# A fused Perceiver block: the last 65 keys of each batch in the first cross-attention, split into 64 keys and one row

## The chip, the core and the metric

The kernel runs on one core of a Trainium2 chip. A core has five engines with a queue of instructions each: TensorE (PE in the profile; PEld is its weight load), VectorE (DVE), ScalarE (ACT), GpSimd (POOL) and SyncE (SP), which here only issues DMAs. ScalarE issues some DMAs too. Each engine runs its instructions in order and waits on semaphores for the others. Products are summed in PSUM, in eight banks of 128 partitions by 512 f32. The metric is the device time of one execution in microseconds, the median over runs.

## The reference

Two layers on a state `x` of 8 batches by 64 queries by 512, with a context of 8 x 1601 keys by 512, all in f32. The first layer has a cross-attention, an attention over low frequencies, and a routed feed-forward; the second a cross-attention, an attention with relative positions, and a feed-forward with quantised weights. The part that the change concerns is the first cross-attention:

```python
HEADS = 16
DIM_HEAD = 64
SCALE = DIM_HEAD ** (-0.5)
q = x @ Wq.T
kv = context @ Wkv.T
k, v = jnp.split(kv, 2, axis=-1)
...
sim = jnp.einsum('bhid,bhjd->bhij', q, k) * SCALE
sim = jnp.where(mask[:, None, None, :], sim, max_neg)
attn = jax.nn.softmax(sim, axis=-1)
out = jnp.einsum('bhij,bhjd->bhid', attn, v)
out = out.transpose(0, 2, 1, 3).reshape(B, Nq, HEADS * DIM_HEAD)
return out @ Wout.T + b_out
```

Keys and values have 16 heads of 64. 1601 keys are twelve blocks of 128 and a last one of 65.

## The kernel before

`l0_xattn` computes this without ever making the keys: the queries are multiplied with the key weights first (`qk`, 512 context channels by 8 heads by 64 queries), so that the scores of a block of keys are context columns times `qk`. Likewise the attention is applied to the context rows, and the value weights come after.

The work goes in 17 steps. Step `2b + half` scores batch `b` for one half of the heads (4 pairs of heads by 2 by 64 queries = 512 score columns, `HALF`; `QH` is 256), and, one step late, `attend` applies the softmax of the step before to the context rows. `outputs` (called by `finish`, after the first pair of blocks of the following step) multiplies with the value weights; every fourth step `project` adds a tile to `x`.

*Scores.* The twelve whole blocks are taken in six pairs. `Run.add` makes seven products instead of eight for each 2 x 2 product of a pair (`Quarters.left` and `right_of` make the sums that this needs, on GpSimd). Each product is a `mul` of two 128 x 128 weights by 256 columns (L512). They go into PSUM tiles `x_ps`, `y_ps`, `z_ps` of two banks each; ScalarE (L460, L491) and VectorE (L465) take them out with the mask's bias added, and VectorE keeps the running maximum `m` over keys (L493).

*The tail.* The 65 last keys are scored at the very start of `scores`: `ctxT_tail` holds 512 channels by 128 columns, of which 65 are loaded and 63 are zero, and four products of 128 x 128 by 512 (L505) give `s_ps`, which ScalarE writes into `s[:, LAST]` (L506). The maximum begins with that block. In `softmax` the last block goes first, and its exponentials land in `tail`, 65 rows of which are used: in the sum (L567) and in `outputs` (L661), with the 65 rows of values `v_tail`.

*Values of the tails.* `values_of_tails`, after step 0, makes the value rows of all 520 tail keys: two halves of 512 value columns by five groups of 104 keys (L233), evacuated by ScalarE and written to the DRAM tile `v_tails`, from which each step loads 65 rows.

*PSUM.* `x`, `y`, `z` and `mm` have two banks each. Everything else goes through the two `mm` banks in the order of the program: `s_ps`, the transposed maxima `m_ps` and `top_ps` (held until the softmax's last subtraction), `vt_ps`, `sum_ps` (the softmax's totals, L645, read by a reciprocal at L647), `v_ps` (L652, L661), `o_ps`, and the products below.

*Queries of the later batches.* Batches 0 and 1 have their `qk` made at the start (`keys_side_of_first`). Those of batches 2 to 7 (`REST`, 384 queries) are made by the generator `keys_side_of_rest` in 40 pieces, while steps 1 to 3 run: per pair of heads `g` one piece for the queries (L291, 128 x 128 by 384), and four with two products of 64 x 128 weights each (L278), stored to the DRAM tile `qk_all`. `some(n)` takes the next `n` pieces: two after each pair in `scores`, `2 * part` after each of the four runs in `attend`, and what is left after step 3. After that, pieces of another generator, which prepares ternary weights, are taken one at a time.

*Queues.* The program is written in the order of its steps, but the instructions of each engine are arranged by a planner, which knows what each waits for and has its own times for them; so products of one step can stand between those of another. Loads go through SP. Its order in a step: `qk` of the step, context columns in six pairs (from the input for half 0, and then written to the DRAM tile `kept`, from which half 1 loads them with their sums), `ctxT_tail` for half 0, and later context rows and values. The six `pair` buffers serve columns and rows alike, so a load of columns waits until rows were used. `piece` has two buffers.

Of the kernel before, what the change touches and what calls it, by code (L numbers as in the profile page):

```python
# [10 lines left out]
F32 = mybir.dt.float32  # L11
BF16 = mybir.dt.bfloat16
U8 = mybir.dt.uint8
# [7 lines left out]
P = 128  # L21
# [120 lines left out]
def l0_xattn(K, x, d, ternary, kept):  # L142
# [7 lines left out]
    with ExitStack() as es:  # L150
# [9 lines left out]
        nc.gpsimd.memset(ones, 1.0)  # L160
        ctxT_tail = wp.tile([P, DC, P], F32, tag="ctxT_tail", name="ctxT_tail")
        nc.gpsimd.memset(ctxT_tail, 0.0)
        bias = wp.tile([P, B, NK], F32, tag="bias", name="bias")
# [45 lines left out]

        v_tails = dp.tile([B * TAIL, 2, HALF], F32, tag="v_tails", name="v_tails")  # L210

        def load_columns_tail(b):
            nc.sync.dma_start(
                ctxT_tail[:, :, :TAIL], d["ctxT"][b, :, LAST * P :].rearrange("(c p) n -> p c n", p=P)
            )
# [5 lines left out]

        def values_of_tails():

            n = B * TAIL // 5
            for half in range(2):
                wvT = load_wvT(half)
                for i in range(5):
                    tails = zp.tile([P, B - 2, 2, S], F32, tag="stage", name="tails", bufs=2)
                    tails = tails.rearrange("p b h q -> p (b h q)")[:, : DC * n].rearrange("p (c n) -> p c n", n=n)
                    nc.sync.dma_start(tails, d["tails"][:, ts(i, n)].rearrange("(c p) n -> p c n", p=P))  # L230
                    ps = ps_m.tile([P, HALF], F32, tag="mm", name="vt_ps")
                    for c in range(DC):
                        nc.tensor.matmul(ps[:n], lhsT=tails[:, c, :], rhs=wvT[:, c, :], start=c == 0, stop=c == DC - 1)  # L233
                    vt = piece([2, HALF], "vt")[:n, 0, :]
                    nc.scalar.copy(vt, ps[:n])
                    nc.scalar.dma_start(v_tails[ts(i, n), half, :], vt)

# [44 lines left out]
        def keys_side_of_rest(xnT):  # L282

            for g in range(NG):
# [8 lines left out]
                nc.scalar.mul(qT, ps, 64**-0.5)  # L293
                yield
                for c in range(DC):
                    pair = [ps_m.tile([P, HALF], F32, tag="mm", name="qk_ps")[:, :REST] for _ in range(2)]
                    keys_side(pair, c, w[:, 1, :], qT)
                    stage = zp.tile([P, B - 2, 2, S], F32, tag="stage", name="stage", bufs=2)
                    for h in range(2):
                        K.copy(stage[:, :, h, :], pair[h].rearrange("p (b q) -> p b q", q=S))  # L300
                    nc.sync.dma_start(
                        qk_all[1][:, :, c, g].rearrange("p b h q -> p b (h q)"),
                        stage.rearrange("p b h q -> p b (h q)"),
                    )
                    yield
# [8 lines left out]

        wqT = sp.tile([P, NK, HALF], F32, tag="s", name="wqT")[:, :8, :].rearrange("p (c j) n -> p c (j n)", j=2)
        wk = sp.tile([P, NK, HALF], F32, tag="s", name="wk")[:, :NG, :]
        def load_weights(j):
# [14 lines left out]
        m32 = wp.tile([B * NK, P], F32, tag="m32", name="m32")  # L332
        nc.scalar.dma_start(m8, d["mask"])
        load_columns_tail(0)
        ctxT = load_columns(0)
        place = [tp.tile([P, 4, 3, QH], F32, tag="pt", name="stage").rearrange("p a b q -> p (a b q)") for _ in range(2)]
        qk = wp.tile([P, DC, HALF], F32, tag="qk", name="qk")
        qT = piece([NG, P], "qT")

        def keys_side_of_first(j):  # L340
# [21 lines left out]
        for j in range(2):  # L362
            ps = bank([P, NG // 2, P], "q_ps")
            for i in range(NG // 2):
                for c in range(DC):
# [6 lines left out]
                    )  # L372
            nc.scalar.mul(qT[:, ts(j, NG // 2), :], ps, 64**-0.5)
            if j == 0:
                for _ in keys_side_of_first(0):
                    pass
                now = qk, right_of(qk, nc.vector)
# [6 lines left out]
            bias.rearrange("p b k -> p (b k)"), ps, 1.0, -MASKED, ALU.subtract, ALU.mult  # L384
        )

        def of_weights():
# [64 lines left out]
        class Scores:  # L452
# [29 lines left out]
            def c21(self, ps):  # L482
                if self.k == LAST - 2:
# [6 lines left out]
                    return  # L490
                nc.scalar.activation(self.s[:, self.k + 1, :QH], ps, AF.Identity, bias=self.bias[1], scale=1.0)  # L491
                for k in (self.k, self.k + 1):
                    nc.vector.tensor_max(self.m, self.m if k else self.s[:, LAST, :], self.s[:, k, :])  # L493

        def scores(b, qkt, ctxT):
            qk, qt = qkt
            s = sp.tile([P, NK, HALF], F32, tag="s", name="s")
            m = tp.tile([P, HALF], F32, tag="m", name="m", bufs=1)
# [3 lines left out]
            }  # L502
            ps = ps_m.tile([P, HALF], F32, tag="mm", name="s_ps")
            for c in range(DC):
                nc.tensor.matmul(ps, lhsT=ctxT_tail[:, c, :], rhs=qk[:, c, :], start=c == 0, stop=c == DC - 1)  # L505
            nc.scalar.activation(s[:, LAST, :], ps, AF.Identity, bias=bias[:, b, LAST : LAST + 1], scale=1.0)  # L506
            run = Run()
            for i in range(NPAIR):
# [15 lines left out]
                if i == 0:  # L524
                    finish()
                if i == 3:
                    project()
# [14 lines left out]

        def softmax(s, top):

            parts = []
            for k in (LAST, *range(0, LAST, 2)):
                n = min(2, NK - k)
                nc.vector.tensor_sub(s[:, k : k + n], s[:, k : k + n], top.unsqueeze(1).to_broadcast([P, n, HALF]))  # L548
                if k == LAST:
                    tail = tp.tile([P, HALF], F32, tag="tail", name="tail")  # L550
                    nc.scalar.activation(tail, s[:, LAST, :], AF.Exp)
                    continue
                nc.scalar.activation(s[:, k : k + n], s[:, k : k + n], AF.Exp)  # L553
# [56 lines left out]
        def attend(b, half, soft, ctx):  # L610
# [3 lines left out]
            v_tail = wp.tile([P, HALF], F32, tag="v_tail", name="v_tail")  # L614
            nc.sync.dma_start(v_tail[:TAIL], v_tails[ts(b, TAIL), half, :])
            parts, total, tail = soft
            run = Run()
            for part, right in enumerate(parts):
                pairs = range(3 * part, 3 * part + 3)
                for m in range(2):  # L620
# [12 lines left out]
                    run.add(mul, Mixed(a, m, part == 0))  # L633
                    some(2 * part)
                    next(aside, None)
# [72 lines left out]
        for step in range(2 * B + 1):  # L708
            if step < 2 * B:
                b, half = divmod(step, 2)  # L710
                if step:
                    now, ctxT = queries_of(b, half), load_columns(b, half)
                    if half == 0:
                        load_columns_tail(b)
                s, m = scores(b, now, ctxT)
                top = top_of(m)
# [7 lines left out]
            if step < 2 * B:  # L724
                before = softmax(s, top)
            if step == 0:
                values_of_tails()
            if step == 3:
# [1675 lines left out]
def layout(i):  # L2404
# [11 lines left out]
        "L0x_WqT": i["L0_xattn_Wq"].T,  # L2416
        "L0x_Wk": wkv[:1024],
        "L0x_WvT": wkv[1024:].T,
        "L0x_Wo": i["L0_xattn_Wout"].T,
# [31 lines left out]
        "c_heads": (np.arange(P)[:, None] // DH == np.arange(32)).astype(np.float32),  # L2451
        "L1x_bp": i["L1_xattn_bp"],
        "tails": i["ctx_1024"][:, LAST * P :].transpose(2, 0, 1).reshape(D, B * TAIL),
        "L1x_ln": np.stack(
# [34 lines left out]
```

## Time and profile before

| | |
|---|---|
| median of 3 runs | 2968.94 us (2965.39 to 2969.26) |
| profiled execution, its time | 2970.64 us |
| its span, first to last instruction | 2968.9 us |
| mean granted TensorE clock | 0.992 |
| busy: PE, PEld, DVE, ACT, POOL | 98%, 72%, 61%, 28%, 29% |
| tail scores L505, 16 steps | 128 instructions, 23.0 to 1316.3 us |
| values of tails L233 | 80 instructions, 71.6 to 113.7 us |
| chain that ended last, by engine | PE 92%, DVE 5%, DMA 1%, ACT 1%, issue 1% |

The span holds the whole program; the first cross-attention runs from 0 to about 1445 us. The profile shows one execution, with starts and lengths of instructions; lengths of neighbouring matmuls overlap because matmuls are pipelined, so the cost of one is the distance between starts. A f32 product appears as two instructions.

### The profile page before, as it was taken

The page shows a single profiled execution, that of the slowest core. Times are in us where ns is not written, and L with a number is a line of the kernel's source. Part 1 is how long each engine was busy: PE and PEld are TensorE (multiplying, and loading weights), DVE is VectorE, ACT ScalarE, POOL GpSimd, SP SyncE. Part 2 cuts the span into 40 slices and gives each one's busy share as a digit, 9 for nine tenths or more (in the row PEclk, how much of TensorE's full clock was granted, in tenths as well). Part 3 has the DMA queues.
Part 4 walks back from the last instruction along what each step waited for, and adds up shares of the span by engine and source line. Part 5 has one row for each costly group of instructions (what it writes and reads, how often), then busy time and mean ns, then how long its engine had stood idle before and what let it go on. Part 6 is the DMA issues. An engine that isn't in the chain of part 4 may idle for free.

```text
span 2968.9 us, 39297 instructions
## 1 busy us (share of the span) xinstructions
PE 2912.2 (98%) x15020; PEld 2145.2 (72%) x15025; DVE 1820.5 (61%) x3057; ACT 836.9 (28%) x1566; POOL 860.9 (29%) x766
## 2 busy tenths in 40 slices
PE   8999999999999999999999999999999999999897
PEld 7677778888888888888554445768677677677664
DVE  4565546666666666666533243587667677676738
ACT  2222322233232222222202222232333323323324
POOL 2232241535435252524010003222413404224011
PEclk9999999999999999999999999999999999999989
DMA  9455565554556564542659974202012021120350
GB/s 337 144 184 172 173 213 182 188 199 128 214 173 225 190 211 164 180 144 95 236 199 351 342 236 150 85 26 78 29 67 80 5 92 42 42 92 11 110 83 15
DMA packets 294699, 436.80 MB, mean 147 GB/s; under 512 B 56248, under 2 KB 192448, under 8 KB 291312
## 3 DMA queue, kind: packets, MB, share of 16 engines
q1 hardware_dynamic: 278153, 393.85, 39.9%
q10 hardware_dynamic: 15719, 38.34, 3.7%
q8 instruction: 119, 1.95, 0.3%
q0 software_dynamic: 640, 2.10, 0.2%
q14 instruction: 68, 0.56, 0.1%
HBM read 357.06 MB, written 77.17 MB: 146 GB/s over the span
## 4 chain that ended last, share of the span: by engine, by line
PE 92%; DVE 5%; DMA 1%; ACT 1%; issue 1%; POOL 0%; POOLq 0%; SPq 0%; DVEq 0%; ACTq 0%
PE x_ps L512 11%; PE x_ps L1580 11%; PE x_ps L624 11%; PE y_ps L1580 8%; PE s_ps L1750 6%; PE z_ps L512 5%; PE z_ps L624 5%; PE h_ps L1264 4%; PE oe_ps L1291 4%; PE acc L1809 3%; PE y_ps L512 3%; PE y_ps L624 3%; PE s_ps L505 2%; PE qk_ps L278 1%; PE vt_ps L233 1%; PE v_ps L652 1%
## 5 line engine op out<-in xcount | busy, mean ns | idle before, releaser
L1640 POOL TENSOR_TENSOR r<-r,minus_half 128x52 f32<-128x52 f32 x32 | 276.9, 8672 | 566.4 <-DVE r L1639 566.4
L512 PE MATMUL x_ps<-qt,ctxT 128*128 128x256 f32 x1152 | 285.2, 381 | 2.5 <-DVE s L465 2.5
L624 PE MATMUL x_ps<-pt,ctx 128*128 128x256 f32 x1152 | 273.9, 380 | 0.7 <-DVE a L602 0.7
L136 POOL TENSOR_TENSOR ctx<-ctx 128x256 f32<-128x256 f32 x96 | 78.7, 819 | 621.8 <-DMA ctx<-in_ctx 475.8
L624 PEld LDWEIGHTS x_ps<-pt,ctx 128*128 128x128 f32 x1152 | 217.9, 190 | 40.4 <-DVE a L602 8.2
L512 PEld LDWEIGHTS x_ps<-qt,ctxT 128*128 128x128 f32 x1152 | 217.3, 190 | 40.9 <-issue 6.3
L1750 PE MATMUL s_ps<-qb,kT 128*128 128x256 f32 x832 | 195.6, 382 | 0.0
L1750 PEld LDWEIGHTS s_ps<-qb,kT 128*128 128x128 f32 x832 | 153.6, 190 | 30.5 <-DVE s L1760 8.1
L493 DVE TENSOR_TENSOR m<-m,s 128x512 f32<-128x512 f32 x144 | 110.4, 767 | 67.7 <-ACT s L491 65.6
L1760 DVE TENSOR_TENSOR s<-s_ps,r 128x512 f32<-128x512 f32 x192 | 127.3, 683 | 17.8 <-PE s_ps L1750 16.7
L548 DVE TENSOR_TENSOR s<-s,top_ps 128x1024 f32<-128x1024 f32 (+1 forms) x112 | 123.0, 1135 | 12.0 <-PE top_ps L540 12.0
L1794 DVE TENSOR_TENSOR s<-s,top_ps 128x1792 f32<-128x1792 f32 x64 | 117.9, 1883 | 16.3 <-PE top_ps L1790 16.3
L566 DVE TENSOR_TENSOR total<-total,s 128x512 f32<-128x512 f32 x160 | 117.1, 732 | 4.6 <-DVE total L566 0.5
L465 DVE SCALAR_TENSOR_TENSOR s<-y_ps,bias,p 128x256 f32<-128x256 f32 x96 | 46.3, 483 | 116.2 <-PE y_ps L512 114.9
L1264 PE MATMUL h_ps<-w,tok 128*128 128x512 f32 x256 | 117.3, 593 | 0.0
L1291 PE MATMUL oe_ps<-w,hT 128*128 128x512 f32 x256 | 115.6, 593 | 0.0
L1547 ACT COPY p<-x_ps 128x256 f32<-128x256 f32 (+1 forms) x80 | 33.1, 414 | 282.7 <-PE x_ps L1580 265.4
L1795 ACT ACTIVATE s<-s 128x1792 f32<-128x1792 f32 x64 | 101.3, 1591 | 38.7 <-DVE s L1794 38.7
L553 ACT ACTIVATE s<-s 128x1024 f32<-128x1024 f32 x96 | 100.7, 1057 | 19.0 <-DVE s L548 14.0
L1283 ACT ACTIVATE hT<-hT_ps,L0f_be,L0f_g 128x128 f32<-128x128 f32 x128 | 55.4, 455 | 179.8 <-PE hT_ps L1282 117.0
L1809 PEld LDWEIGHTS acc<-s,v 128*64 128x64 f32 x1664 | 92.3, 139 | 18.3 <-issue 17.0
L1809 PE MATMUL acc<-s,v 128*64 128x128 f32 x1664 | 102.9, 278 | 0.0
(470 smaller groups left out, 6055.3 us busy)
## 6 DMA issues: line engine op xcount, KB each, us to landing
w<-in_L0f_W SPq DMA_DIRECT2D x64, 1024.0 KB
ctx<-in_ctx SPq DMA_DIRECT2D x192, 256.0 KB
kept<-ctxT SPq DMA_DIRECT2D x48, 896.0 KB
ctxT<-kept SPq DMA_DIRECT2D x48, 896.0 KB
ctxT<-kept SPq DMA_DIRECT2D x16, 2688.0 KB
ctxT<-in_ctxT SPq DMA_DIRECT2D x96, 256.0 KB
wvT<-in_L0x_WvT SPq DMA_DIRECT2D x18, 1024.0 KB
qk<-qk_all SPq DMA_DIRECT2D x15, 1024.0 KB
```

Source lines behind the costliest of these rows:

```text
L512: nc.tensor.matmul(ps, lhsT=ctxT[i][:, Quarters.LEFT[n], ts(e, P)], rhs=right[n][:, e, :], start=start and e == 0, stop=e == 1, skip_group ...
L548: nc.vector.tensor_sub(s[:, k : k + n], s[:, k : k + n], top.unsqueeze(1).to_broadcast([P, n, HALF]))
L566: nc.vector.tensor_add(total, total if k > 1 else s[:, 0, :], s[:, k, :])
L624: nc.tensor.matmul(ps, lhsT=ctx[pair][:, Quarters.LEFT[n], ts(m, P)], rhs=right[n][:, i, :], start=start and i == 0, stop=i == 2, skip_gro ...
L1264: nc.tensor.matmul(ps, lhsT=self.tok[:, c, :], rhs=self.w1[n][:, c, :], start=c == 0, stop=c == DC - 1)
L1291: nc.tensor.matmul(ps, lhsT=self.hT[:, f, :], rhs=self.w2[f // 4][:, f % 4, :], start=f == 0, stop=f == 15)
L1580: nc.tensor.matmul(ps, lhsT=left(n, e), rhs=right(n, e), start=start and e == 0, stop=e == 1, skip_group_check=not start,)
L1640: nc.gpsimd.tensor_tensor(r, r, minus_half, ALU.pow)
L1750: nc.tensor.matmul(ps[:, i].rearrange("p h q -> p (h q)"), lhsT=kT[c][:, ts(k0 + i, P)], rhs=qb[c].rearrange("p h q -> p (h q)"), start=Tr ...
L1760: nc.vector.tensor_mul(out, ps, by)
L1794: nc.vector.tensor_sub(part, part, top.to_broadcast([P, n, 2 * P]))
L1809: product = nc.tensor.matmul(acc[ds(64 * j, 64), c, :], lhsT=v[:, k, ds(c * P + 64 * j, 64)], rhs=s[:, k, ts(j, P)], start=k == 0, stop=k ...
```

## The change

The tail's 65 keys become 64 keys and one row, the 1601st key of each batch.

- `tail_scores`: for batches 1 to 7 the 64 keys are scored in products of 64 columns of weights by 256, the first half of the score columns into partitions 0 to 63 of the bank and the second into 64 to 127. Two activations bring both into the step's `tail` tile. Batch 0 keeps one product of 65 keys by 512. The block moves from the start of `scores` to after `finish` in the first pair (for batch 0 it stays at the start). There is no `s[:, LAST]` any more; `tail` (three buffers) is made per step, and the running maximum takes it in after the third pair.
- The 1601st rows: `keys_of_left`, after step 0, makes the key vectors of the eight 1601st rows (`left`), transposes them into `kkT`, with one head of each pair in the upper 64 partitions and the other in the lower, zero elsewhere, and multiplies them with the queries of batch 1 (`qT1`, copied aside by GpSimd). A new piece of `keys_side_of_rest` does so with the queries of batches 2 to 7, for each pair of heads (80 columns of weights by 384, of which 16 rows are kept). `keep_rows` adds the mask's bias `row_bias` and writes them to the DRAM tiles `rows`; `load_row` brings a step's 512 scores of the 1601st key into partition 64 of `tail`, for batches 1 to 7. The products are made for all eight keys and all batches; only those of a batch with itself are loaded.
- `values_of_tails`: 64 keys a batch, four groups of 128 instead of five of 104 per half, and the values of the eight 1601st rows as products of 8 columns by 256.
- `some(2)` after every run of `attend`.

```diff
-        ctxT_tail = wp.tile([P, DC, P], F32, tag="ctxT_tail", name="ctxT_tail")
-        nc.gpsimd.memset(ctxT_tail, 0.0)
+        ctxT_tail = wp.tile([P, DC, TAIL], F32, tag="ctxT_tail", name="ctxT_tail")
...
+        nc.gpsimd.memset(kkT, 0.0)
...
-        def values_of_tails():
-
-            n = B * TAIL // 5
+        def values_of_tails(left):
...
-                for i in range(5):
+                for i in range(B // 2):
...
-                        nc.tensor.matmul(ps[:n], lhsT=tails[:, c, :], rhs=wvT[:, c, :], start=c == 0, stop=c == DC - 1)
-                    vt = piece([2, HALF], "vt")[:n, 0, :]
-                    nc.scalar.copy(vt, ps[:n])
-                    nc.scalar.dma_start(v_tails[ts(i, n), half, :], vt)
+                        nc.tensor.matmul(ps, lhsT=tails[:, c, :], rhs=wvT[:, c, :], start=c == 0, stop=c == DC - 1)
+                    vt = piece([2, HALF], "vt")[:, 0, :]
+                    nc.scalar.copy(vt, ps)
+                    for j in range(2):
+                        nc.scalar.dma_start(v_tails[2 * i + j, :H2, half, :], vt[ts(j, H2)])
+                ps = ps_m.tile([P, QH], F32, tag="mm", name="vl_ps")
+                for c in range(DC):
+                    for n in range(2):
+                        nc.tensor.matmul(
+                            ps[ds(n * H2, B)],
+                            lhsT=left[:, c, :],
+                            rhs=wvT[:, c, ts(n, QH)],
...
+                nc.scalar.dma_start(v_tails[:, H2, half, :], vt)
+
+        ROWS = H2 + 2 * B
+
+        def rows_of(g):
+            return kkT[:, ds(2 * B * g, ROWS)]
+
+        def keys_of_left(left, qT):
+
+            ps = ps_m.tile([P, HALF], F32, tag="mm", name="kl_ps")
+            for c in range(DC):
+                wkT = piece([2, HALF], "wkT")
+                nc.sync.dma_start(wkT, d["L0x_WkT"][ts(c, P), :].rearrange("p (n k) -> p n k", n=2))
+                for n in range(2):
+                    nc.tensor.matmul(
+                        ps[ds(n * H2, B)], lhsT=left[:, c, :], rhs=wkT[:, n, :], start=c == 0, stop=c == DC - 1
+                    )
+            kk = piece([2, HALF], "kk")[:B]
+            for n in range(2):
+                nc.scalar.copy(kk[:, n, :], ps[ds(n * H2, B)])
+            ps = ps_m.tile([P, NG, B], F32, tag="mm", name="kkT_ps")
+            for g in range(NG):
+                nc.tensor.transpose(ps[:, g, :], kk[:, g // 4, ts(g % 4, P)], K.ident[:B, :B])
+            at = kkT[:, :P].rearrange("p (g h b) -> p g h b", h=2, b=B)
+            for h in range(2):
+                nc.vector.tensor_copy(at[ds(h * H2, H2), :, h, :], ps[ds(h * H2, H2)])
+            ps = ps_m.tile([P, NG, S], F32, tag="mm", name="row_ps")
+            for g in range(NG):
+                nc.tensor.matmul(ps[:ROWS, g, :], lhsT=rows_of(g), rhs=qT[:, g, :], start=True, stop=True)
+            keep_rows(ps[: 2 * B].rearrange("p g q -> p (g q)"), rows[0].rearrange("h b g c q -> (h b) (g c q)"))
+
+        def keep_rows(ps, out):
+
+            t = zp.tile([P, HALF], F32, tag="rows", name="rows")[: 2 * B, : ps.shape[-1]]
+            nc.scalar.activation(t, ps, AF.Identity, bias=row_bias, scale=1.0)
+            nc.scalar.dma_start(out, t)
+
+        def load_row(tail, b, half):
+            r = rows[b > 1][:, b, ts(half, NG // 2), b - (2 if b > 1 else 1), :]
+            nc.sync.dma_start(
+                tail[H2:TAIL].rearrange("p (g h q) -> p g h q", h=2, q=S), r.rearrange("h g q -> g h q").unsqueeze(0)
+            )
...
                 nc.scalar.mul(qT, ps, 64**-0.5)
                 yield
+                ps = ps_m.tile([P, HALF], F32, tag="mm", name="row_ps")[:, :REST]
+                nc.tensor.matmul(ps[:ROWS], lhsT=rows_of(g), rhs=qT, start=True, stop=True)
+                keep_rows(ps[: 2 * B], rows[1].rearrange("h b g c q -> (h b) g (c q)")[:, g])
+                yield
...
+        r8 = wp.tile([2 * B, 1], U8, tag="r8", name="r8")
+        for h in range(2):
+            nc.scalar.dma_start(
+                r8[ts(h, B)], d["mask"].rearrange("(b k) n -> b k n", k=NK)[:, LAST, H2 : H2 + 1]
+            )
...
+        nc.scalar.dma_start(left, d["left"].rearrange("(c p) b -> p c b", p=P))
...
+            nc.gpsimd.tensor_copy(qT1[:, ts(j, NG // 2), :], qT[:, ts(j, NG // 2), S:])
...
+        nc.vector.tensor_copy(row_bias, r8)
+        nc.vector.tensor_scalar(row_bias, row_bias, 1.0, -MASKED, ALU.subtract, ALU.mult)
...
+                if self.k == 0:
+                    nc.vector.tensor_max(self.m, self.s[:, 0, :], self.s[:, 1, :])
+                    return
...
-            ps = ps_m.tile([P, HALF], F32, tag="mm", name="s_ps")
-            for c in range(DC):
-                nc.tensor.matmul(ps, lhsT=ctxT_tail[:, c, :], rhs=qk[:, c, :], start=c == 0, stop=c == DC - 1)
-            nc.scalar.activation(s[:, LAST, :], ps, AF.Identity, bias=bias[:, b, LAST : LAST + 1], scale=1.0)
+
+            def tail_scores():
+                ps = ps_m.tile([P, HALF], F32, tag="mm", name="s_ps")
+                at = bias[:, b, LAST : LAST + 1]
...
+                for c in range(DC):
+                    for n in range(2):
+                        nc.tensor.matmul(
+                            ps[ds(n * H2, H2), :QH],
+                            lhsT=ctxT_tail[:, c, :H2],
+                            rhs=qk[:, c, ts(n, QH)],
+                            start=c == 0,
+                            stop=c == DC - 1,
+                        )
+                for n in range(2):
+                    nc.scalar.activation(
+                        tail[:H2, ts(n, QH)], ps[ds(n * H2, H2), :QH], AF.Identity, bias=at[:H2], scale=1.0
+                    )
+
+            if b == 0:
+                tail_scores()
...
                 if i == 0:
                     finish()
+                    if b:
+                        tail_scores()
+                if i == 2:
+                    nc.vector.tensor_max(m[:TAIL], m[:TAIL], tail[:TAIL])
...
-                    some(2 * part)
+                    some(2)
...
+                tail = tp.tile([P, HALF], F32, tag="tail", name="tail", bufs=3)
+                if b:
+                    load_row(tail, b, half)
...
-                values_of_tails()
+                values_of_tails(left)
+                keys_of_left(left, qT1)
```

New inputs are laid out for this: the transposed key weights, the eight 1601st rows, and the 64 tail keys of each batch side by side.

## The prediction

> **What bounds the kernel now.** I read the page's 40 slices first, then busy time by stage, then what TensorE waited for, then its timeline around the tail block.
>
> Page, the span in 40 slices of 74 us:
>
> ```profile
> PE   8999999999999999999999999999999999999897
> DVE  4565546666666666666533243587667677676738
> PEclk9999999999999999999999999999999999999989
> ```
>
> The change touches slices 0 to 19 only. There TensorE is at 9 throughout, at its full clock, and VectorE at 4 to 6.
>
> Busy time by stage (columns: length, then PE, PEld, DVE, ACT, POOL with instructions, granted clock, DMA share, GB/s):
>
> ```profile
> 69.00:118.00 49.00, 47.39 (x134) 22.78 (x133) 26.18 (x33) 14.58 (x23) 5.03 (x4) 1.00 0.50 150
> 118.00:408.00 290.00, 289.12 (x1401) 217.80 (x1399) 166.60 (x272) 78.34 (x159) 100.82 (x127) 1.00 0.54 171
> 408.00:1433.00 1025.00, 1021.58 (x5515) 861.82 (x5516) 658.45 (x1044) 275.13 (x538) 403.70 (x484) 1.00 0.52 179
> ```
>
> TensorE lacks 1.6 us in 49, 0.9 in 290 and 3.4 in 1025. VectorE is busy 64% of the last stretch, DMA 52%. The waits of TensorE after 408 us say the same:
>
> ```profile
> PE x_ps L512 <- DVE s L465: 1.6, 3, 0.7
> PE m_ps L535 <- DVE m L480: 0.8, 1, 0.8
> PE x_ps L624 <- DVE a L602: 0.7, 2, 0.6
> PE s_ps L505 <- ACT stage L52: 0.3, 1, 0.3
> ```
>
> So 3.4 us of waits in twelve steps: here a microsecond of TensorE work is a microsecond of span, until something else comes last. Timeline of TensorE at the border of two steps (start, length, instructions):
>
> ```profile
> 574.54 2.74 PE L505 MATMUL s_ps<-qk,ctxT_tail 128*128 128x512 f32 x6
> 577.12 1.03 PE L512 MATMUL x_ps<-qk,ctxT 128*128 128x256 f32 x4
> ...
> 580.57 1.03 PE L512 MATMUL z_ps<-qk,ctxT 128*128 128x256 f32 x4
> 581.53 0.65 PE L645 MATMUL sum_ps<-total,ones 128*64 128x256 f32 x4
> 582.01 0.63 PE L652 MATMUL v_ps<-a,wvT 128*64 128x64 f32 x16
> ...
> 584.23 0.29 PE L661 MATMUL v_ps<-tail,v_tail 65*64 65x64 f32 x4
> 584.44 1.13 PE L512 MATMUL x_ps<-qk,ctxT 128*128 128x256 f32 x4
> ```
>
> Lengths overlap, so I cost by starts. Each f32 product is two instructions (L505 has 128 in 16 steps: 8 for 4 products). Six of L505 take 577.12 - 574.54 = 2.58 us, 0.43 each; a 256-wide one is half, 0.216. L645 is the row that decides: 64-column weights, 256 wide, two products into partitions 0-63 and 64-127, as the new tail block. Its four instructions take 582.01 - 581.53 = 0.48 us where one after another would be 4 x 0.216 = 0.864. The two column halves do run together, at 0.556 of the serial time.
>
> **The change, part by part.**
>
> *Tail scores, steps 2 to 15.* Out: 8 x 0.432 = 3.46 us. In: 16 instructions, 256 wide, at 0.12 (L645) = 1.92. Saved 1.54 a step, 14 steps: **-21.5 us**. Bounds: best, perfect overlap, 16 x 0.108 + 0.05 = 1.78, saving 23.5; worst by L1809 (64-column products with changing weights, 18 in 1.19 us where serial is 18 x 0.107 = 1.92, ratio 0.62): 2.14, saving 18.4. I take L645, nearest in shape. Steps 0 and 1 keep 65 columns by 512: no gain.
>
> The switch between whole-array and 64-column work shows at L645 and after L661: z_ps ends at 580.57 + 0.86 = 581.43, L645 starts 0.10 later; L661 should end near 584.35 and L512 starts 0.1 after. The new block stands behind L661, between switches that exist already: 0; if put elsewhere, 0.2 a step, 2.8 in all. The Trainium skill, TensorEngine Tiling (Array Packing), section Tiling Modes, says that changing the mode drains the array, which speaks against the change; the trace agrees and prices a drain at about 0.1 us. By that rule with two more drains a step the sum below would end 2.8 us higher, by the row alone as it stands.
>
> *Values of the tails (L233).* 80 instructions of 0.431 (40 take 114.58 - 97.35 = 17.23) become 64: **-6.9**. The 1601st rows' values: per half 4 x 2 products, 8 columns, 256 wide: 32 instructions at 0.12 = **+3.8** (bounds 3.5 perfect overlap, 6.9 none; 8 columns isn't in this trace, the 32-column L1627 has 8 instructions of 384 in 0.89 us against 2.59 serial, so some overlap is sure).
>
> *Keys of the 1601st rows.* 16 instructions, 512 wide, at 0.24: **+3.8** (3.5 to 6.9). Eight transposes at 0.11 (L535 and L540: four in 0.44 to 0.48): +0.9. Eight row products, 64 wide: 16 at 0.06 (L278's first ones, 64 in 3.84) to 0.11 (L911, 16 in 1.7): +1.4. Together **+6.1**.
>
> *Rows for batches 2 to 7.* Eight products of 80 columns by 384: 16 at 0.323 (L291: 8 in 2.58): **+5.2**.
>
> TensorE in all: -21.5 - 6.9 + 3.8 + 6.1 + 5.2 = **-13.3 us**.
>
> *What must stay hidden.* ScalarE: two activations of 64x256 (0.47, L491) for one of 0.69; eight row evacuations of about 0.5; 8 more v_tails issues at 0.31: under 13 us, at 27% busy in the long stretch. VectorE: as many maxima as before (tail's now 65 partitions at i = 2, 0.69 by L567's 65x512), no change. POOL: two copies of 128x256 for qT1 (0.72 to 1.17, L136); the first falls before POOL's first sums at 19.5, the second delays column sums that take 4.4 us a pair against some 7 of TensorE: 0. SP: fourteen load_row issues of 0.4 behind the column loads and the kept writes; TensorE needs a row only after VectorE's maximum at i = 2, about 20 us into scores. SP's last kept issue stands near 588 in the step that starts at 574.5, the maximum after 592: only some 4 us spare in steps with half 0, cut short by earlier products. A late row holds VectorE, and behind it c11 and c12, whose banks TensorE needs two products later; three waits of 1 us would be 3 us. I take 0, bounds 0 to 7 (seven batches by 1 us). row_bias: two small VectorE operations; if they stand ahead of the statistics at 3.94 and their bytes, issued two 0.65 us slots after L333's, come late, the start slips by up to 1.7; I take 0.
>
> *The chain of the left keys.* Four 512 KB weight loads through two buffers, each pair after TensorE frees the last; 1 MB took 97.35 - 91.74 = 5.6 us (wvT), so 2.8 to 5.6 each round, two rounds, then copies (2 x 0.59), transposes, copies, row product: about 13 us in which TensorE has 6 of this work. Cover: products of step 1, of which only some 6 us each were taken in the gaps at 75 and at 91.5 to 97.3 and more than 25 remain; the wait for wvT there cost 0.47 us. I take +1, bounds 0 to 13.
>
> *The reciprocal.* The tail block is the third user of a two-bank ring after sums and v_ps, so it waits until VectorE's 1.76 us reciprocal (L647, 582.23) has read sums. It ends at 583.99, v_ps at 584.35: spare 0.36. But the scores now start 3.4 us earlier against VectorE's leftovers of the last softmax, which ran until 579.4 here: L465 twice and the reciprocal then end near 582.2 where v_ps ends near 581.8. I take 0.1 a step, **+1.4** (0 to 0.5, 7 us).
>
> *Pacing.* Two pieces in every part of attend instead of 0 and 2 exhaust all 48 pieces by step 3; before, 4 of 40 were left for the burst at 400 to 408, where qk_ps waited 0.61 for a stage copy: **-0.5**. One mm bank is held by top_ps early in attend, so pieces may bunch; the 290 us stretch wastes only 0.9 now: 0, up to 3.
>
> Sum: -13.3 + 1 + 1.4 - 0.5 = **-11.4 us**. The profiled execution is 2970.64 us with a span of 2968.9; -11.4 gives 2959.2. The median of the runs is 2968.94, 1.7 lower: 2957.5 there.
>
> **Rivals.**
>
> 1. *The head isn't covered*: the left keys' chain stands in TensorE's order without products between. +12 on the sum: +0.6, 2969.5. For: these products share a ring of two mm banks with step 1's tail, and SP's buffers are waited for. Against: the same region waits 0.47 for a 5.6 us load now.
>
> 2. *Slower: the reciprocal becomes the border's bound.* If VectorE puts leftovers (four pt operations of 0.95, total adds of 0.73) ahead of it so that it begins when v_ps is done, TensorE stands 1.76 us at every tail block: 14 x 1.76 = 24.6 in place of 1.4, +11.8: 2980.7. Above 0.9 us a step the gain is gone, above 1.35 it is slower than can be doubted. Against: VectorE had 1.25 us idle just before it, and the order was good enough for 3.4 us of waits in twelve steps.
>
> 3. *No overlap in the new block*: 64-column products one after another save nothing (16 x 0.216 = 3.46), and the 8-column ones cost 3.1 more twice: -11.4 + 21.5 + 6.2 = +16.3, 2985. Against: L645 and L1809.
>
> 4. *TensorE is no longer the bound*: a shorter step is given back to loads of columns (SP waits for TensorE's pairs) or late rows, about 0.5 us a step: -4.4, 2964.5. Against: 64% and 52% busy.
>
> **How the numbers follow.** Forecast 0.64 (own range 2952 to 2963: tail at its bounds, head 0 to 4), head 0.13, reciprocal 0.13, no overlap 0.04, given back 0.06. Less than 0.2% (5.9 us) can't be told from no change here. Faster: 0.64 and 0.04 of a half-covered head, 0.68. Same: 0.09 head, 0.04 small reciprocal waits, 0.06 given back, 0.19. Slower: 0.13. The range 2950 to 2970 leaves some 0.05 below (perfect overlap everywhere and a better order) and 0.15 above.
>
> **What would show it.** Right: the tail block's 16 instructions in 1.8 to 2.0 us, L233's successor 64 long, 16 row products near 0.32, TensorE waits of the first 1433 us below 15 us in all, the step about 1.5 us shorter. Wrong: s_ps waiting for the reciprocal in most steps (rival 2), kl_ps or kkT_ps waiting over 5 us (1), the block at 3.4 us (3), VectorE held by a tail row from SP (4).

## The result and the profile after

The changed kernel takes 2962.44 us (median of 20 runs, 2959.84 to 2966.47) against 2968.57 for the kernel before beside it (20 runs, 2963.67 to 2973.43): ratio 0.9983, 95% interval 0.9976 to 0.9989. That is 6.1 us between the medians and 5.0 by the ratio (3.3 to 7.1 by the interval), where 11.4 were forecast: faster, since the interval leaves out 1, inside the range, and about half the size. It stands at the edge of the 5.9 us below which the prediction spoke of no change, and by the number alone rival 4 (4.4 us) would fit as well as the forecast; only the marks below tell them apart. The profiled execution is 2962.59 us with a span of 2960.8.

The page of the changed kernel, the same slices as before:

```profile
PE   8999999999999999999999999999999999999897
DVE  4465456676766666666533243588667677676747
```

TensorE is as full as it was. So the question is not whether it was the bound, but what it now does or waits for beyond the sum. I read that from marks: the start of the first transpose of the maxima, `m_ps`, in each step, taken from TensorE's timeline in each run. The row `next stage` is the first product behind the cross-attention, and the three rows under it are differences. "Second profile" is that of the changed kernel run again, below. All are starts in us:

| mark | before | after | after, second profile |
|---|---|---|---|
| step 0 | 69.22 | 69.52 | 69.56 |
| step 1 | 147.79 | 153.63 | 154.96 |
| step 4 | 449.22 | 455.53 | 457.55 |
| step 15 | 1357.80 | 1351.43 | 1351.65 |
| next stage (`xl_ps`) | 1446.31 | 1439.88 | 1440.11 |
| from step 0 to 1 | 78.57 | 84.11 | 85.40 |
| from step 1 to 4 | 301.43 | 301.90 | 302.59 |
| from step 4 to 15 | 908.58 | 895.90 | 894.10 |

The head loses 5.8 to 7.2 us, steps 2 to 4 come out even or up to 1.2 longer (tail block against the rows of the later batches), and eleven steps win 12.7 to 14.5, some 1.2 to 1.3 each instead of 1.54. At the end of the cross-attention 6.2 to 6.4 us are left, which is what the medians show.

Timeline of TensorE at a border, the step shown before (L744, L751, L760, L590 are the former L645, L652, L661, L505):

```profile
583.26 0.65 PE L744 MATMUL sum_ps<-total,ones 128*64 128x256 f32 x4
583.75 0.64 PE L751 MATMUL v_ps<-a,wvT 128*64 128x64 f32 x16
...
585.96 0.29 PE L760 MATMUL v_ps<-tail,v_tail 65*64 65x64 f32 x4
586.65 1.95 PE L590 MATMUL s_ps<-qk,ctxT_tail 128*64 128x256 f32 x16 [0.40 <-DVE rs L746]
588.53 1.13 PE L609 MATMUL x_ps<-qk,ctxT 128*128 128x256 f32 x4
```

The block's 16 instructions take 588.53 - 586.65 = 1.88 us, where L505 took 3.46. But L760 starts its last four at 585.96, they need some 0.12, and the block comes 0.57 later, waiting for the reciprocal L746. VectorE in the same place, before and after:

```profile
575.16 0.95 DVE L559 TENSOR_TENSOR pt<-s 128x768 f32<-128x768 f32 x1
...
577.88 1.53 DVE L562 TENSOR_TENSOR pt<-s,pt 128x768 f32<-128x768 f32 x1
579.98 0.48 DVE L465 SCALAR_TENSOR_TENSOR s<-y_ps,bias,p 128x256 f32<-128x256 f32 x1 [0.57 <-PE y_ps L512]
581.71 0.48 DVE L465 SCALAR_TENSOR_TENSOR s<-z_ps,bias,u 128x256 f32<-128x256 f32 x1 [1.25 <-PE z_ps L512]
582.23 1.76 DVE L647 RECIPROCAL rs<-sum_ps 128x256 f32<-128x256 f32 x1
```

```profile
579.99 0.42 DVE L707 TENSOR_TENSOR a<-x_ps,a 128x256 f32<-128x256 f32 x1 [1.80 <-PE x_ps L723]
580.33 0.95 DVE L658 TENSOR_TENSOR pt<-s 128x768 f32<-128x768 f32 x1
581.20 0.95 DVE L660 TENSOR_TENSOR pt<-s 128x768 f32<-128x768 f32 x1
582.06 0.95 DVE L659 TENSOR_TENSOR pt<-s,pt 128x768 f32<-128x768 f32 x1
582.93 0.48 DVE L538 SCALAR_TENSOR_TENSOR s<-y_ps,bias,p 128x256 f32<-128x256 f32 x1
583.33 1.21 DVE L661 TENSOR_TENSOR pt<-s,pt 128x768 f32<-128x768 f32 x1
584.46 0.47 DVE L538 SCALAR_TENSOR_TENSOR s<-z_ps,bias,u 128x256 f32<-128x256 f32 x1
584.85 1.74 DVE L746 RECIPROCAL rs<-sum_ps 128x256 f32<-128x256 f32 x1
```

The four `pt` operations left over from the softmax end at 584.5 now, 1.2 us after the totals were started; before, they ended at 579.4, 2.1 us ahead of them. So the two L538, which waited for their products before (L465: 0.57 and 1.25 us), now follow without a gap. The reciprocal starts 0.9 us after its totals are done (583.26 + 0.65 against 584.85) and ends 0.5 us after `v_ps`.

### The profile page after: what moved, and what is told of

It reads as the page before. It is cut to its first block, busy times and chain, and to the rows that moved or that the text cites. A ratio compares the mean times of both kernels' runs of the same rounds, so it can differ in the third digit from the quotient of the medians.

```text
span 2960.8 us, 39781 instructions
## 1 busy us (share of the span) xinstructions
PE 2898.2 (98%) x15209; PEld 2137.2 (72%) x15209; DVE 1818.9 (61%) x3061; ACT 847.2 (29%) x1593; POOL 861.8 (29%) x768
## 4 chain that ended last, share of the span: by engine, by line
PE 89%; DVE 6%; DMA 2%; issue 1%; ACT 1%; POOL 0%; SPq 0%; ACTq 0%; POOLq 0%; DVEq 0%
PE x_ps L723 11%; PE x_ps L609 11%; PE x_ps L1683 11%; PE y_ps L1683 8%; PE s_ps L1853 6%; PE z_ps L723 5%; PE z_ps L609 5%; PE h_ps L1367 4%; PE oe_ps L1394 4%; PE acc L1912 3%; PE y_ps L723 3%; PE y_ps L609 2%; PE qk_ps L336 1%; PE sum_ps L1730 1%; PE o_ps L779 1%
## 5 line engine op out<-in xcount | busy, mean ns | idle before, releaser
L569 DVE TENSOR_TENSOR m<-m,s 128x512 f32<-128x512 f32 x128 | 99.5, 777 | 53.2 <-ACT s L564 51.2
L651 DVE TENSOR_TENSOR s<-s,top_ps 128x1024 f32<-128x1024 f32 x96 | 113.1, 1208 | 0.0
L538 DVE SCALAR_TENSOR_TENSOR s<-y_ps,bias,p 128x256 f32<-128x256 f32 x96 | 46.3, 482 | 104.2 <-PE y_ps L609 104.2
L652 ACT ACTIVATE s<-s 128x1024 f32<-128x1024 f32 x96 | 100.5, 1057 | 16.8 <-DVE s L651 12.2
```

## The experiments

Times are medians; the ratio is to the kernel before, run beside. That kernel took 2968.57, 2966.53, 2967.74 and 2965.94 us in the four series of runs, so a microsecond or two between times of different series says nothing; there the ratios count, and the marks.

**One after another.** All products of the 64 keys go to partitions 0 to 63.

```diff
                 for c in range(DC):
-                    for n in range(2):
-                        nc.tensor.matmul(
-                            ps[ds(n * H2, H2), :QH],
-                            lhsT=ctxT_tail[:, c, :H2],
-                            rhs=qk[:, c, ts(n, QH)],
...
+                    nc.tensor.matmul(ps[:H2], lhsT=ctxT_tail[:, c, :H2], rhs=qk[:, c, :], start=c == 0, stop=c == DC - 1)
...
```

> The changed kernel with its 64 tail keys scored by products of 64 columns by 512 that all go to partitions 0 to 63, so that none can run beside another. Theory A (the gain is the overlap of two column halves): the block goes from 1.88 us to 8 x 0.43 = 3.45 us in each of 14 steps, +1.57 each, +22 us, to about 2984 us, slower than the kernel before by some 16 us. Rival B (the gain comes from the new place of the block, or from whatever the planner made of the rest): little change, under +8 us.

Measured: 2983.5 us, ratio 1.0057 (1.0040 to 1.0073), 21 above the changed kernel. From step 4 to 15 it takes 912.97, 17.1 more, 1.55 a step. In its timeline the block has half the instructions, each twice as wide:

```profile
591.02 0.29 PE L753 MATMUL v_ps<-tail,v_tail 65*64 65x64 f32 x4
591.83 3.65 PE L589 MATMUL s_ps<-qk,ctxT_tail 128*64 128x512 f32 x8 [0.53 <-DVE rs L739]
```

Theory A holds: the whole gain is that two halves of 64 columns run side by side. Without it the change loses 17 us against the kernel before. This prices the block's part of rival 3, for which 21.5 us were worked out; the 8-column products, its other part, still run side by side here.

**Totals copied out.** ScalarE empties the bank, VectorE inverts from SBUF.

```diff
-            nc.vector.reciprocal(rs, sums)
+            nc.scalar.copy(rs, sums)
+            nc.vector.reciprocal(rs, rs)
```

> The changed kernel; ScalarE copies the totals out of PSUM (about 0.37 us) and VectorE takes the reciprocal from there, so the bank that the tail block needs comes free more than a microsecond earlier. Theory A (the tail block stands behind the 1.76 us reciprocal): after v_ps the block starts without a wait in all 14 steps, the stretch from the first maximum of step 4 to that of step 15 gets 2.2 us shorter (895.9 to 893.7), time -2 us. Rival B (TensorE only waits elsewhere instead, VectorE being late at the border of the steps whatever the bank): that stretch stays within 0.5 us.

Measured: 2958.21 us, ratio 0.9968 (0.9956 to 0.9979). From step 4 to 15: 891.23, 4.7 less than the first profile of the changed kernel and 2.9 less than the second. The reciprocal stands as late as before on VectorE, and the block no longer minds:

```profile
584.23 1.74 DVE L747 RECIPROCAL rs<-rs 128x256 f32<-128x256 f32 x1
...
585.33 0.29 PE L761 MATMUL v_ps<-tail,v_tail 65*64 65x64 f32 x4
585.44 1.90 PE L590 MATMUL s_ps<-qk,ctxT_tail 128*64 128x256 f32 x16
587.27 1.13 PE L609 MATMUL x_ps<-qk,ctxT 128*128 128x256 f32 x4
```

Theory A, by more than the waits that the profile names (1.5 us as idle TensorE, 4.2 as waits of its weight loads): the border got 0.3 to 0.4 us shorter, eleven times over. Against the kernel before, the eleven steps now win 908.58 - 891.23 = 17.35 us, 1.58 each, which is what the block alone saves; so nothing else of that size is lost in these steps.

**Without the later rows.** The products of the 1601st keys with the queries of batches 2 to 7 are left out.

```diff
-                nc.tensor.matmul(ps[:ROWS], lhsT=rows_of(g), rhs=qT, start=True, stop=True)
-                keep_rows(ps[: 2 * B], rows[1].rearrange("h b g c q -> (h b) g (c q)")[:, g])
...
-            r = rows[b > 1][:, b, ts(half, NG // 2), b - (2 if b > 1 else 1), :]
+            r = rows[0][:, b, ts(half, NG // 2), 0, :]
...
```

> The changed kernel without the products that make the 1601st rows of batches 2 to 7 (16 instructions of 80 columns by 384), their evacuations and stores; every step loads a row of batch 1's queries in their place. Theory A (they cost what they occupy on TensorE): the stretch from the first maximum of step 1 to that of step 4 gets 5.2 us shorter (301.9 to 296.7), time -5.2. Rival B (their place in the two-bank ring costs more than they occupy): -7 or more. Rival C (they fill what would be idle): under -3.

Measured: 2957.36 us, ratio 0.9968 (0.9955 to 0.9980). From step 1 to 4: 297.26, 4.6 less (5.3 against the second profile). Theory A: they cost what they occupy; in the changed kernel the 16 instructions take 0.323 each, 5.2 in all.

**Without the left keys.** Beyond that, no key vectors of the 1601st keys and no rows of batch 1; a step loads values of `x` in place of its row, so this kernel doesn't compute the block.

```diff
-                keys_of_left(left, qT1)
...
+            nc.sync.dma_start(tail[H2:TAIL], d["x"][b : b + 1, :])
...
```

> As the run without later rows, and the key vectors of the 1601st keys and batch 1's rows aren't made either; a step's row is 512 values of the input x. Theory A (the head costs 3.84 + 0.69 + 1.13 us of TensorE work, and 1.3 us of waits for weights and 1.5 us of switches and gaps between its pieces on top): the stretch from the first maximum of step 0 to that of step 1 gets 8.5 us shorter (84.1 to 75.6), the time 13.7 us shorter than the changed kernel, 2949. Rival B (its waits are covered, only the products count): the stretch gets 5.7 us shorter.

Measured: 2950.63 us, ratio 0.9943 (0.9927 to 0.9960). From step 0 to 1: 76.04, which is 8.1 and 9.4 below the two profiles. Theory A. The time fell by 11.8; the 13.7 expected were the sum of two stretches, and the very start of this execution took 1.5 us more (see the last section). The 8 to 9 us are more than the 5.66 us of products, and the changed kernel's timeline in the head shows the rest:

```profile
118.87 1.03 PE L267 MATMUL kl_ps<-wkT,left 128*8 128x512 f32 x4
119.83 1.13 PE L609 MATMUL x_ps<-qt,ctxT 128*128 128x256 f32 x4
121.52 1.03 PE L267 MATMUL kl_ps<-wkT,left 128*8 128x512 f32 x4 [0.55 <-DMA wkT<-in_L0x_WkT]
...
124.84 1.03 PE L267 MATMUL kl_ps<-wkT,left 128*8 128x512 f32 x4
...
127.66 1.03 PE L267 MATMUL kl_ps<-wkT,left 128*8 128x512 f32 x4 [0.73 <-DMA wkT<-in_L0x_WkT]
```

Four pieces of 0.96 us stand between products of step 1: two wait for weights, 1.3 us in all, and the products after a piece start 0.1 later than the columns need, as at the other switches. The second profile waits 0.40 and 1.22 us for these weights, and 1.41 for `wvT`, for which the first doesn't wait; that is the 1.3 us by which the two differ in this stretch:

```profile
97.69 14.00 PE L235 MATMUL vt_ps<-wvT,tails 128*128 128x512 f32 x32 [1.41 <-DMA wvT<-in_L0x_WvT]
```

**Block at the start.** `tail_scores` stands ahead of the first pair again, for all batches.

```diff
-            if b == 0:
-                tail_scores()
+            tail_scores()
             run = Run()
...
-                    if b:
-                        tail_scores()
```

> The changed kernel with the tail block at the start of scores again, as before, for all batches. Theory A (placed behind v_ps the block shares its switches with the products around it but waits for the reciprocal): the wait goes (-2.2 to -4.7 us from the maximum of step 4 to that of step 15, which took 895.9), and the planner splits the block in two of three and five products between products of the whole array, four switches of 0.1 a step (+4.4) and one more end without a partner (0.2 a step, +2.2): between -1 and +4 us in that stretch. Rival B (the block gave VectorE cover at the border, which its new place took away): -4 us or more.

Measured: 2972.3 us, ratio 1.0016 (1.0007 to 1.0026), slower than before. From step 4 to 15: 901.33, 5.4 to 7.2 more than the changed kernel. That lies beyond the range of A, and away from B. Its timeline at the same border:

```profile
581.67 1.08 PE L590 MATMUL s_ps<-qk,ctxT_tail 128*64 128x256 f32 x6
582.68 1.56 PE L720 MATMUL x_ps<-pt,ctx 128*128 128x256 f32 x6
584.17 1.51 PE L590 MATMUL s_ps<-qk,ctxT_tail 128*64 128x256 f32 x10
585.61 1.13 PE L608 MATMUL x_ps<-qk,ctxT 128*128 128x256 f32 x4
```

The planner cuts the block behind its third product. The two parts take 1.01 and 1.44, 2.45 instead of 1.88. That fits a part with an odd number of products ending with a half alone (4 x 0.117 + 2 x 0.216 = 0.90 and 8 x 0.117 + 2 x 0.216 = 1.37). Four switches come on top, between products of the whole array and products of 64 columns: L720 should hold the array for 6 x 0.216 = 1.30 and holds it for 1.49, two switches of 0.1, and the products before the first part and behind the second take 0.1 longer each. So 0.57 for the cut and 0.4 for the switches are 10.7 us in eleven steps; less the reciprocal's 2.9 to 4.7, that makes 6.0 to 7.8, against 5.4 to 7.2 measured.

The Trainium skill, TensorEngine Tiling (Array Packing), section Tiling Modes, says that a change of mode drains the array. The trace agrees, with about 0.1 us each time, and the place of the block decides whether it is paid.

**Weights ahead.** Two of the four weight pieces go into the tile `a`, free until the first `attend`.

```diff
+            early = tp.tile([P, DC, HALF], F32, tag="a", name="wkT", bufs=1)
             for c in range(DC):
-                wkT = piece([2, HALF], "wkT")
+                wkT = early[:, ts(c, 2), :] if c < 2 else piece([2, HALF], "wkT")
```

> The changed kernel; two of the four pieces of key weights for the 1601st keys go into a buffer that is free until the first attend, so all four can be loaded without waiting for a product. Theory A (in the head 1.3 us are waits for these weights and part of the gaps are switches, one run of pieces less here): the stretch from the first maximum of step 0 to that of step 1 goes from 84.1 to about 82.3. Rival B (the waits only move to the evacuation chain behind, kk, transposes, copies, row product): within 0.5 us.

Measured: 2962.31 us, ratio 0.9983 (0.9974 to 0.9993). From step 0 to 1: 84.73, between the two profiles of the changed kernel (0.6 above one, 0.7 below the other). Nothing was gained, as rival B has it, but not for its reason. The waits for these weights fell from 1.3 to 0.3 us, and no product of the evacuation chain waits. TensorE waits for two other loads instead, for `wvT` 0.67 us and for the `qk` of step 1:

```profile
76.70 1.10 PE L610 MATMUL x_ps<-qk,ctxT 128*128 128x256 f32 x4 [1.28 <-DMA qk<-qk_all]
```

The two weights that no longer wait for a buffer are issued at 53.23 us, ahead of the columns and of this load. That they hold it back is likely, but no run tests it.

**Three mendings.** Copied totals, weights ahead, and the bytes of the 1601st keys' mask through SP, behind the first columns.

```diff
...
-            nc.scalar.dma_start(
+            nc.sync.dma_start(
                 r8[ts(h, B)], d["mask"].rearrange("(b k) n -> b k n", k=NK)[:, LAST, H2 : H2 + 1]
...
```

The reason lies at the start of the changed kernel, where VectorE converts these bytes ahead of the first statistics' variance:

```profile
6.52 0.14 DVE L457 CAST row_bias<-r 16x1 f32<-16x1 uint8 x1 [1.48 <-DMA r<-in_mask]
6.59 0.13 DVE L56 TENSOR_SCALAR lt_var<-lt_mv 128x1 f32<-128x1 f32 x1
...
8.06 1.11 PE L329 MATMUL xt_ps<-ident,xn 128*128 128x128 f32 x4 [8.06 <-DVE xn L82]
```

The first transposes stood at 6.38 before:

```profile
6.38 1.12 PE L271 MATMUL xt_ps<-ident,xn 128*128 128x128 f32 x4 [6.38 <-DVE xn L82]
```

> The changed kernel with the totals copied out by ScalarE, two pieces of key weights loaded ahead, and the mask bytes of the 1601st keys loaded through SP after the columns, so that VectorE's conversion of them no longer stands ahead of the first statistics. Theory A (all three are losses that the changed kernel has beside its product work): first transposes at 6.4 us instead of 8.1, the stretch of step 1 about -2, the stretch from step 4 to step 15 near 891.2, the time 7 us below the changed kernel, near 2955. Rival B (they are not additive; one wait takes the place of another): 2958 or more.

Measured: 2961.63 us, ratio 0.9978 (0.9969 to 0.9987); rival B. The first transposes are at 6.32 and the steps from 4 to 15 take 889.64, as theory A has it, and from step 0 to 1 it takes 83.09, 1.0 to 2.3 less. But step 0's maximum comes at 74.34, some 5 us late. The later load holds VectorE in the middle of step 0:

```profile
39.48 0.75 SPq L401 DMA_DIRECT2D r<-in_mask  x2
43.12 0.14 DVE L458 CAST row_bias<-r 16x1 f32<-16x1 uint8 x1 [3.92 <-DMA r<-in_mask]
44.58 2.08 PE L337 MATMUL qk_ps<-qT,wk 64*128 64x128 f32 x14 [3.40 <-DVE stage L50]
```

The wait wasn't removed but moved, and made longer.

**Two mendings.** Copied totals; the conversion on ScalarE, from the early load.

```diff
-        nc.vector.tensor_copy(row_bias, r8)
-        nc.vector.tensor_scalar(row_bias, row_bias, 1.0, -MASKED, ALU.subtract, ALU.mult)
+        masked = wp.tile([2 * B, 1], F32, tag="masked", name="masked")
+        nc.gpsimd.memset(masked, MASKED)
+        nc.scalar.copy(row_bias, r8)
+        nc.scalar.activation(row_bias, row_bias, AF.Identity, bias=masked, scale=-MASKED)
```

> The changed kernel with the totals copied out by ScalarE, and the mask bytes of the 1601st keys turned into the bias by ScalarE, which has nothing to do before 15 us, from the same early load. Theory A (the conversion on VectorE stood ahead of the first statistics, and the run with three mendings lost that gain because its later load held VectorE at 39 to 43 us): first transposes at 6.4 us, first tail products about 1.6 us earlier than the changed kernel's, the stretch from step 4 to step 15 near 891, the time 4 to 7 us below that of the changed kernel beside it. Rival B (the start is bound by the loads of the query weights, so an earlier start buys nothing): 4 us below, as with the copied totals alone.

Measured: 2956.58 us (2951.01 to 2961.89), ratio 0.9967 (0.9955 to 0.9979). The next stage starts at 1431.08, 15.2 before the first kernel and 9 before the changed one. First transposes:

```profile
6.39 1.11 PE L329 MATMUL xt_ps<-ident,xn 128*128 128x128 f32 x4 [6.39 <-DVE xn L82]
7.61 0.19 ACT L459 CAST row_bias<-r 16x1 f32<-16x1 uint8 x1
```

ScalarE takes up the bytes while nobody waits. The first transposes and the steps from 4 to 15 (888.54) are as theory A has them; the first tail products come at 22.63 against 23.50 and 23.54, 0.9 earlier and not 1.6. The time is 4.9 us below the changed kernel beside it, and six of its seven runs lie below all twelve of that one. But the copied totals alone have the same ratio, 0.9968, so the times don't show what the conversion on ScalarE adds, and between A and B they don't decide. Of the 4.2 us by which the next stage starts earlier than with the copied totals alone (1435.24), 2.7 lie between steps 4 and 15, where the two kernels do the same.

**The changed kernel again**, beside the last run:

> The changed kernel as it is, for comparison on the same chip: ratio to the kernel before near 0.998, first maximum of step 1 near 153.6 us, stretch from step 4 to step 15 within 1 us of 895.9 if these stretches are as steady as they looked in the other runs.

Measured: 2961.46 us, ratio 0.9984 (0.9975 to 0.9992); marks in the table above. The stretch from step 0 to 1 differs by 1.3 us between two executions of the same kernel, and the one from 4 to 15 by 1.8, so smaller differences there say nothing; from step 12 to 15 three steps agree to 0.2.

**Values as before**, five groups of 104:

```diff
-                for i in range(B // 2):
+                for i in range(5):
...
```

> The changed kernel with the values of the tails made as before, five groups of 104 rows a half, 1601st rows among them, instead of four of 128 and the products of 8 columns. Theory A (that part of the change saves 34.5 - 27.9 - 3.7 us): the stretch from the first maximum of step 0 to that of step 1 goes from 84.1 to 87.0. Rival B (it saves nothing, the stretch being set by the chain of loads): within 1 us.

Measured: the stretch takes 87.94, 2.5 to 3.8 more: theory A (2.9). Its only time, 2975.57, isn't comparable: behind the cross-attention, where nothing differs, that execution took 1530.7 us instead of 1520.9.

## Why the prediction came out as it did

- **The bound** was right: TensorE stayed full, each product taken out or put in showed in full (the 21 us of one after another, the later rows, the left keys), and rival 4, gains given back to loads, didn't come: no wait for a tail row or for columns appears among TensorE's waits, nor among VectorE's a wait for a row.
- **Tail block**: -1.54 a step forecast, 1.92 us long; measured 1.88 long, 20.61 us for eleven where before they took 37.77: -1.56. Over 14 steps -21.8.
- **Values**: -6.9 + 3.8 forecast; the 64 instructions take 27.9, the 8-column ones 3.66 (0.114 each, overlapping as fully as 64 columns): -3.0.
- **Later rows**: +5.2 forecast, 4.6 to 5.3 measured.
- **The chain of the left keys** was mis-sized: +6.1 and +1 for waits, 7.1 in all. The products were cheaper (3.84 + 0.69 + 1.13 = 5.66), what lies between them dearer: the stretch is 8.1 to 9.4 shorter without them, so some 3 us are not products, and 1.3 of these are waits for weights. I had counted switches for the block and not for pieces strewn among whole-array products. Rival 1 in small.
- **The reciprocal** was mis-sized most: +1.4 forecast (0.1 a step, bounds to 7). Its removal brings 2.9 to 4.7 from step 4 to 15 alone, 0.3 to 0.4 a step. The mechanism was worked out rightly: counted from the maximum of the step before (537.14 before, 541.96 after), VectorE's leftovers end at 42.3 and 42.6 us, as late as assumed, while the totals start at 44.4 and 41.3. The working gave a reciprocal that ends 0.4 us after `v_ps` (582.2 against 581.8), and 0.5 was measured at this border; but the sum took 0.1 a step, and no reason is given for it. That is the term that failed most. Rival 2's mechanism came at a third to a half of its decisive 0.9 us a step.
- **row_bias** I costed at nothing, with 1.7 as the bound: the first transposes came 1.7 late. Of that 0.4 is left at the first tail products in both profiles of the changed kernel, and 0.2 to 1.9 over all nine profiles that convert on VectorE at the start (last section).
- **Pacing**: -0.5 forecast, and not to be seen. Step 4 lost its burst (94.86 to 90.9), but the pieces went into steps 2 and 3, which grew by some 2 us each. From step 1 to 4 the three blocks save 4.9 and the later rows cost 5.2, together +0.3; measured +0.5 and +1.2.

With measured sizes: -21.8 - 3.0 + 5 + 8.7 + 4 + 0.2 to 1.9 = -5.2 to -6.9 us, against 6.1 between the medians. So the mechanism and the sign were right, and half the gain went into three small waits and gaps that the order of engines made. One of them, the reciprocal's, could be taken away with a gain in time; the conversion of the mask bytes could be moved with a gain in the marks alone; the waits for weights only changed their place.

## What to carry to other kernels

Where one engine is full, a change that saves its work by a quarter of a per cent is decided by what its new pieces wait for: for each moved block, name the user of its bank just before, and follow that engine's queue from the same border, not from the old timeline. When a working gives a wait, put that wait into the sum, not a smaller one. A small conversion of late bytes on an engine that the critical chain uses can cost their landing time (1.7 us at the first transposes here); an engine that is idle is a better place than a later load. Pieces of 64 or fewer columns of weights are cheap beside others of that kind and cost some 0.1 us at each border with whole-array work, and they should come in even numbers.

## What the hardware showed beyond that

The first 32 instructions of L366 (later L436), 16 products, take 5.31 to 6.75 us, and the same 32 in their second group 3.84, while the granted clock reads 1.00 in both. Within the first group the rate changes once: in the changed kernel's profile nine of them lie between 9.96 and 12 us and twelve in the one microsecond from 14 to 15. The change comes near 14 us in the kernel before and near 13 in the changed one (starts 8.28 and 9.96), but after 15 in the kernel without the left keys (start 10.01, 6.75 long). So a start that is 1.7 us later costs anything from 0.2 to 1.9 us at the first tail products, against the one profile of the kernel before. What sets the rate wasn't tried.

Sixteen single mask bytes, issued at 1.43 us, were there at about 6.5; the 13 KB of the whole mask, issued at 0.74, at 4.0 in the same execution.

Products of 8 columns in two halves run side by side like those of 64: 0.114 us an instruction for 256 columns, where one of the whole array takes 0.216.
